# Selective scan in four layers: state tiles of four quarters of n by 32 channels instead of two halves by 64

## The chip, the cores and the metric

The kernel runs on one core of a Trainium2 chip. The metric is the device time of one launch, in microseconds (us); lower is better. The engines are named as in the profile: PE (TensorE matmul), PEld (TensorE weight load), DVE (VectorE), ACT (ScalarE), POOL (GpSimd), SP (SyncE, which here issues every DMA).

## The reference

An image of 8 x 64 x 64 x 96 passes through four layers, each `x = x + f(groupnorm(x))`. Each `f` projects 96 channels to 2 x 192, runs a depthwise convolution with SiLU over the first 192, then a selective scan over the L = 4096 positions with n = 16 states per channel, and after a layer norm (not in the last layer) and a gate `silu(z)` projects 192 channels back to 96. In the first three layers the scan runs in four directions (rows, columns, and each backwards; in the second layer rows and columns are walked in serpentine order) and the results are added. In the fourth it runs once. Cut to what matters here:

```python
dts, Bs, Cs = split(x_proj @ xs)               # rank, 16, 16 rows for each position
delta = softplus(dt_proj @ dts + dt_bias)      # 192 channels
def step(h, (u_t, d_t, b_t, c_t)):             # h is 192 channels x 16 states
    h = exp(d_t[..., None] * A) * h + (d_t * u_t)[..., None] * b_t[None, :]
    y = einsum('dn,n->d', h, c_t)
    return h, y
y = scan(step) + D * xs
```

## The kernel before, in words

The outermost loop runs over the 8 images of the batch, and inside it the four layers are written out. A layer has three stages: the convolution stage (`layer`, up to `by_columns`), the scan stage (`scans`), and the norm stage (`z`, `center`, `spread_`, `norm_`, `out`, `residual`). Everything is fp32, and PE runs each such product as two matmul records.

The scan stage walks chunks of 512 positions: 32 chunks in the first three layers (four directions of eight) and 8 in the last, so 104 for each image and 832 in all. A chunk holds 192 x 16 = 3072 scans of 512 positions, that is 24 scan instructions of 128 rows ("units"). In the kernel before, a unit's 128 rows are two halves of n by 64 channels: rows 0 to 63 hold one state for 64 channels, rows 64 to 127 the state eight further on for the same channels. Four units make a state tile `h` of 128 x 4 x 512; a chunk has `RS` = 6 such tiles, walked as two groups g of four states by three channel tiles t.

For each chunk the work is:

- `project`, `keep_x_dbl`: x_proj on PE gives rank, B and C rows. C and, for the backward directions, all rows go to memory. `load_x_dbl` reads them back there.
- `turn_v`, `softplus`, `delta_of`, `turn_u`, `du_of`: delta and delta*u with positions on the rows (`delta_t`, `du_t`), on PE, ACT, POOL and DVE.
- `spread_b`, `diagonals`: B goes through memory into a 128 x 64 x 64 tile `diag` whose blocks are diagonal matrices of B.
- `turn_back`, `keep_delta`: delta back with channels on the rows. Each of three 64-channel parts is copied from PSUM to one half of a 128 x 512 tile by ACT, and a DMA copies that half to the other half of the rows.
- `enter(q)`: the products `(delta*u)^T diag`, which give delta*u*B for two units at once in a two-bank PSUM tile `dbu`: 16 products with 64 x 64 weights and 128 moving columns each. Two such PSUM tiles exist.
- `decay(m)`: ACT forms exp(delta * A) for unit m, into one of six `d_a` buffers.
- `scan(m)`: DVE runs the recurrence of unit m over 512 positions (`tensor_tensor_scan`).
- `keep(s)`, `read_out(s)`: ACT keeps the last column of a finished state tile, and POOL multiplies the 128 x 2048 tile by C in place. C stands in `cs[i, g]`, two tiles of 1 MB for a chunk, filled by eight DMAs of `spread_c` that repeat each C row over 64 partitions. For the very last tile of a layer DVE does the product in four pieces.
- `add_up(i, e)`: PE sums over n with a 0/1 matrix `sel` of 128 x 64, each time 512 columns, into two PSUM banks `y_ps`; 24 products for a chunk.
- `close_sums(i, o)`: DVE adds `y_ps` to the layer's result, in the order of the direction.

The order on every engine is written out by hand. The loop over m (one m for each unit) emits, in this order: `keep` and `read_out` at every fourth m, `enter(m//2+1)` at every even m, `scan(m)`, `decay(m+4)`, `add_up` at every fourth m, and then what the table `plan` has for the slot `m % 24`. The table places the preparation of the next chunk and the closing of the last; slots are named below as in it. `SL` = 24 slots make a chunk:

```python
        if slot % 4 == 3:
            of, e = divmod(m - 15, SL)
            if 0 <= of < len(walk):
                add_up(of, e // 2)
                add_up(of, e // 2 + 1)
        for do, ahead, *rest in plan.get(slot, ()):
```

All DMAs stand in SP's one queue in program order. The start of a layer's scans (`first_project` to `first_load`) is interleaved with the convolution stage, where `by_two` builds three convolution chunks by pairs of an ACT product (tile `more`, taken by `piece` from the pool `delta` of six buffers) and a POOL addition.

Of the kernel before, what the change touches and what calls it, by code (L numbers as in the profile page):

```python
# [32 lines left out]
NT = 3  # L33
NJ = 8
# [11 lines left out]
NEGMEAN, CEN_B, ONE, EPS, N_CONST = 352, 416, 480, 481, 482  # L46
# [73 lines left out]
def kernel(ctx: ExitStack, tc: tile.TileContext, x_in, const_in, *rest):  # L120
# [3 lines left out]
    def pool(name, bufs, space=None):  # L124
# [9 lines left out]
        cpool=pool("c", 3),  # L134
        upool=pool("u", 4),
        deltas=pool("delta", 6),
# [40 lines left out]
def layer(tc, env, x, stats, x_of, x_to, n, ly):  # L177
# [23 lines left out]
    def piece(name):  # L201
        return env.deltas.tile([128, CH], F32, tag="delta", name=name)
# [329 lines left out]
    with set_of("natural_log_exp_and_others"):  # L532
# [15 lines left out]
        env.cpool.tile([128, 4, CH], F32, tag="c", name="gates"),  # L548
# [147 lines left out]
def scans(tc, env, n, ly, w, u_mem, u_first, d, neg_a, make_ys, two_banks, wide):  # L696
# [9 lines left out]
    sel = const[:, SEL : SEL + 64]  # L706
# [3 lines left out]
    RS, SL = 6, 24  # L710
    halves = [slice(0, 64), slice(64, 128)]
# [14 lines left out]

    def place(s):

        i, r = divmod(s, RS)
        return i, r // NT, r % NT  # L730

# [6 lines left out]
    def u_of(i, half):  # L738
        return u_first(half, 0) if i == 0 else us[i][0 : (128, 64)[half], half, :]

    def load_u(i, part):
        if i >= len(walk):
            return
        k, c = walk[i]
        if part == 0:
            us[i] = env.upool.tile([128, 2, CH], F32, tag="u", name="u")
        s = slice(c * CH, (c + 1) * CH)
        if part == 0:
            nc.sync.dma_start(us[i][:, 0, :], u_mem[k % 2][0:128, s])
        else:  # L750
            nc.sync.dma_start(us[i][halves[part - 1], 1, :], u_mem[k % 2][128:DI, s])

    def project(i, half):
# [8 lines left out]
        for e in range(2):  # L762
            rows = slice(0, 128) if half == 0 else halves[e if i > 1 else 0]
            u = u_first(half, walk[i][1]) if i < 2 else us[i][rows, half, :]
            nc.tensor.matmul(  # L765
                dbls[i][:, e],
                w[rows, at : at + ly.x_rows],
                u[:, e * CH // 2 : (e + 1) * CH // 2],
                start=half == 0,
                stop=half == 1,  # L770
            )

    def keep_x_dbl(i):
# [14 lines left out]
        if i > 1:  # L788
            there = env.deltas.tile([128, CH], F32, tag="delta", name="x_hi")[64 : 64 + XP]
# [17 lines left out]
    def spread_c(i, g, part):  # L807
        k, c = walk[i]
        if part == 0:
            cs[i, g] = env.cpool.tile([128, NH, CH], F32, tag="c", name="c")  # L810
        half, pair = divmod(part, 2)
        rows, js = slice(64 * half, 64 * half + 64), slice(2 * pair, 2 * pair + 2)
        n0 = half * NJ + g * NH + 2 * pair
        of = c_mem[k][n0 : n0 + 2, c * CH : (c + 1) * CH]
        nc.sync.dma_start(cs[i, g][rows, js], of.partition_broadcast(64))
# [5 lines left out]
    def turn_v(i, b):  # L821


        if b == 0:
            for name in ("delta_t", "du_t"):
                turned[i, name] = env.turned.tile([128, NB4, DI], F32, tag=name, name=name)
# [13 lines left out]
    def turn_u(i, b, half):  # L840
# [5 lines left out]
        for b_ in (b, 2 + b):  # L846
# [3 lines left out]
            else:  # L850
                at = halves[b_ // 2 if i > 0 else 0]
                u = us[i][at, 1, :] if i > 0 else u_of(i, 1)
                nc.tensor.transpose(to[:, 128:DI], block(b_, u), ident[at, at])  # L853

    def softplus(i, part):

        v = turned[i, "v"][:, :, 0:DI]
        if part == 0:
            rests[i] = env.turned.tile([128, NB4, DI], F32, tag="rest", name="rest", bufs=1)
# [38 lines left out]
    def turn_back(i, o, part):  # L898
# [3 lines left out]
        for b in (2 * part, 2 * part + 1):  # L902
            of = turned[i, "delta_t"][:, b]
            for half in range(o + 1 if i == 0 else 1):
                to = deltas[i, "ps"][64 * half : 64 * half + 128 // (o + 1), o]
                of_ = of[:, 0:128] if o == 0 else of[:, 128:DI]
                if half == 0:
                    nc.tensor.transpose(block(b, to), of_, ident)  # L908
                else:
                    nc.tensor.matmul(block(b, to), of_, ident, start=True, stop=True)  # L910

    def keep_delta(i, t):

        delta = env.deltas.tile([128, CH], F32, tag="delta", name="delta")
        if i > 0:
            here = halves[t % 2]
            nc.scalar.copy(delta[here], deltas[i, "ps"][here, t // 2])  # L917
            nc.sync.dma_start(delta[halves[1 - t % 2]], delta[here])
        elif t == 2:
            nc.scalar.copy(delta, deltas[i, "ps"][:, 1])  # L920
        else:
            for half in range(2):
                of = deltas[i, "ps"][64 * t : 64 * t + 64, 0]
                nc.scalar.copy(delta[64 * half : 64 * half + 64], of)
        deltas[i, t] = delta


    def enter(q):
# [4 lines left out]
        i, g, t = place(s)  # L933
# [3 lines left out]
        for b in range(NB4):  # L937
            for e in range(2):
                rows = slice(64 * e, 64 * e + 64)
                for half in range(2):  # L940
                    at = b * NS + g * NJ + half * NH + 2 * pair
                    nc.tensor.matmul(  # L942
                        to[64 * half : 64 * half + 64, e, b],
                        du[rows, b, 64 * t : 64 * t + 64],
# [6 lines left out]
    def decay(m):  # L951
# [4 lines left out]
        i, g, t = place(s)  # L956
        d_a = env.decays.tile([128, CH], F32, tag="d_a", name="d_a")
        at = (walk[i][0] * NT + t) * NJ + g * NH + m4
        nc.scalar.activation(d_a, deltas[i, t], AF.Exp, scale=neg_a[:, at : at + 1])  # L959
        decays[m] = d_a  # L960

    def scan(m):
        s, m4 = divmod(m, NH)
        i, g, t = place(s)
# [6 lines left out]
        j = t * NJ + g * NH + m4  # L971
# [10 lines left out]
    def keep(s):  # L982

        i, g, t = place(s)
        at = t * NJ + g * NH
        last = 0 if walk[i][0] >= 2 else CH - 1
        nc.scalar.copy(states[i // NCH][:, at : at + NH], hs[s][:, :, last])  # L987

    def read_out(s):
        i, g, t = place(s)  # L990
        if s < n_s - 1:
            nc.gpsimd.tensor_tensor(hs[s], hs[s], cs[i, g], ALU.mult)  # L992
            return
        for m4 in range(NH):
            of = hs[s][:, m4]
            nc.vector.tensor_tensor(of, of, cs[i, g][:, m4], ALU.mult)

    def add_up(i, e):


        g, e = divmod(e, 6)
        if g == 0 and e == 0:
            sums[i] = [env.ps_y.tile([128, CH], F32, tag=f"y{o}", name=f"y{o}_ps") for o in range(2)]
        s = i * RS + g * NT
        if e < 4:
            work = [(0, 0, s, e), (0, 1, s + 1, e)]
        else:
            work = [(1, 0, s + 2, e - 4), (1, 1, s + 2, e - 2)]
        for o, half, of, state in work:
            nc.tensor.matmul(  # L1010
                sums[i][o][64 * half : 64 * half + 64],
                sel,
                hs[of][:, state, :],
                start=g == 0 and e in (0, 4),
                stop=g == 1 and e in (3, 5),
# [3 lines left out]
    def close_sums(i, o):  # L1019
# [3 lines left out]
        u_ = us[i][:, o, :].rearrange("p (o i) -> p o i", i=W)  # L1023
# [23 lines left out]
        5: [(turn_u, 1, 1, 0), (turn_u, 1, 1, 1)],  # L1047
# [4 lines left out]
        11: [(keep_delta, 1, 2), (close_sums, -1, 0)],  # L1052
        14: [(close_sums, -1, 1)],
# [6 lines left out]
    for at, (do, *what) in (  # L1060
        *((5 + 3 * part, (spread_c, 0, part)) for part in range(4)),
        *((18 + 3 * part, (spread_c, 1, part)) for part in range(4)),
        *((a + 6 + a // 2, (diagonals, a, 1)) for a in range(8)),
    ):
        plan.setdefault(at % SL, []).append((do, 1 - at // SL, *what))
    for part, at in enumerate((1, 2, 4)):
# [15 lines left out]
    def first_softplus(between=lambda: None):  # L1082
# [3 lines left out]
        for part in range(4):  # L1086
            spread_c(0, 0, part)
# [11 lines left out]
    def first_delta():  # L1099
        for t in range(NT):  # L1100
            keep_delta(0, t)

    def first_load():
# [3 lines left out]
        for part in range(4):  # L1107
            spread_c(0, 1, part)
# [10 lines left out]
    for m in range(-8, (len(walk) + 1) * SL):  # L1119
# [10 lines left out]
        if slot % 4 == 3:  # L1130
            of, e = divmod(m - 15, SL)
            if 0 <= of < len(walk):
                add_up(of, e // 2)
                add_up(of, e // 2 + 1)
# [7 lines left out]
def constants():  # L1142
    a = np.zeros((128, N_CONST), np.float32)
    for p in range(128):
        a[p, SEL + p % 64] = 1
        a[p, IDENT + p] = 1
# [11 lines left out]
def pack(ly, conv_w, win, conv_b, x_proj, dt_w, dt_b, a_log, d, w_out, gamma=None, beta=None):  # L1158
# [6 lines left out]
    for k in range(K):  # L1165
# [14 lines left out]
        for half in range(2):  # L1180
            for j in range(NJ):
                a[NS + half * NJ + j, at + DI + j // NH * NJ + half * NH + j % NH] = 1
        a[64 : 64 + XP, at : at + DI + NS] = a[0:XP, at : at + DI + NS]
    a_log = a_log.reshape(K * NT, 64, 2, NJ).transpose(2, 1, 0, 3).reshape(128, -1)
# [55 lines left out]
```

## Time and profile before

| | us |
|---|---|
| median of 3 runs | 29361.2 (29357.19 to 29361.32) |
| the profiled execution, its own time | 29331.35 |
| its span, first to last instruction | 29329.6 |
| mean granted PE clock | 0.98 |

| engine | busy us | share of the span | instructions |
|---|---|---|---|
| PE | 27127.0 | 92% | 391056 |
| DVE | 27395.8 | 93% | 26841 |
| POOL | 25414.1 | 87% | 7101 |
| ACT | 19839.6 | 68% | 35728 |

The shares are averages over three kinds of stage. From the first scan of a layer to the last, the trace has 25195 us in the sum over 32 layers (8 images by 4); the remaining 4135 us lie in the convolution and norm stages. Busy time is the union of an engine's instruction spans; matmul records overlap each other, so a busy PE isn't PE at its peak. The 16 DMA engines are 49% busy in the mean, nearly all of it on SP's queue.

### The profile page before, as it was taken

How to read it: one execution, taken by the hardware profiler on the slowest of the kernel's cores; microseconds unless marked ns; L12 is line 12 of the kernel's file. 1: busy time of each engine (PE TensorE's matmuls, PEld its weight loads, DVE VectorE, ACT ScalarE, POOL GpSimd, SP SyncE). 2: the span in 40 equal slices, each digit the busy share in tenths (PEclk: the TensorE clock that was granted, in tenths of full speed). 3: DMA queues.
4: the chain of work that ended last, by engine and by line, in shares of the span. 5: the costliest groups of instructions: out<-in, count | busy, mean ns of one | idle time of the engine just before them, and what ended most of it. 6: DMA issues, size and time to landing. Idle time of an engine off the chain costs nothing. (4 is left out here: it accounts for less than half of the span.)

```text
span 29329.6 us, 919486 instructions
## 1 busy us (share of the span) xinstructions
PE 27127.0 (92%) x391056; PEld 15249.2 (52%) x391056; DVE 27395.8 (93%) x26841; ACT 19839.6 (68%) x35728; POOL 25414.1 (87%) x7101
## 2 busy tenths in 40 slices
PE   9999999999999999999999999999999999999999
PEld 5555455554555545555455554555545555455554
DVE  9999899998999989999899998999989999899998
ACT  6667666676666766667666676666766667666676
POOL 8898788987889878898788987889878898788987
PEclk9999999999999999999999999999999999999999
DMA  5444454454544545445454454544545455454454
GB/s 132 117 117 125 106 131 117 117 125 106 131 116 118 125 107 130 118 118 125 106 132 117 116 126 107 131 117 116 125 106 131 116 117 125 106 132 117 116 126 106
DMA packets 1947780, 3498.19 MB, mean 119 GB/s; under 512 B 448400, under 2 KB 469264, under 8 KB 1920624
## 3 DMA queue, kind: packets, MB, share of 16 engines
q1 hardware_dynamic: 1943664, 3438.91, 47.7%
q8 instruction: 3120, 51.12, 0.8%
q14 instruction: 996, 8.16, 0.1%
HBM read 2787.17 MB, written 302.84 MB: 105 GB/s over the span
## 5 line engine op out<-in xcount | busy, mean ns | idle before, releaser
L992 POOL TENSOR_TENSOR h<-h,c 128x2048 f32<-128x2048 f32 x4960 | 22450.1, 4567 | 44.5 <-ACT state L987 37.6
L973 DVE TENSOR_TENSOR_SCAN h<-d_a,state,dbu 128x512 f32<-128x512 f32 x17472 | 20778.0, 1274 | 13.0 <-PE dbu L942 6.0
L959 ACT ACTIVATE d_a<-delta,neg_a 128x512 f32<-128x512 f32 x19968 | 13372.2, 719 | 428.1 <-DVE h L973 390.9
L942 PE MATMUL dbu<-diag,du_t 64*64 64x128 f32 x319488 | 11236.9, 275 | 1631.8 <-DVE h L973 1606.6
L942 PEld LDWEIGHTS dbu<-diag,du_t 64*64 64x64 f32 x319488 | 8881.1, 131 | 6556.5 <-issue 5591.6
L1010 PE MATMUL y_ps<-h,const 128*64 128x512 f32 x39936 | 9697.2, 605 | 13.3 <-POOL h L992 13.3
L1010 PEld LDWEIGHTS y_ps<-h,const 128*64 128x64 f32 x39936 | 2441.1, 136 | 3802.9 <-issue 3757.3
L987 ACT COPY state<-h 128x4 f32<-128x4 f32 x4992 | 974.6, 195 | 3692.8 <-DVE h L973 3687.3
L973 DVE TENSOR_TENSOR_SCAN h<-d_a,dbu 128x512 f32<-128x512 f32 x2496 | 2838.3, 1201 | 348.9 <-PE dbu L942 227.6
L877 POOL TENSOR_TENSOR delta_t<-delta_t,rest 128x768 f32<-128x768 f32 x832 | 1525.5, 1834 | 1835.3 <-ACT state L987 1508.3
L917 ACT COPY delta<-delta_ps 64x512 f32<-64x512 f32 x2400 | 1392.3, 580 | 1716.2 <-PE delta_ps L908 1677.1
L832 PE MATMUL v<-w,x_dbl 39*128 39x208 f32 (+1 forms) x5120 | 1388.4, 475 | 33.3 <-ACT x_dbl L781 33.3
L480 POOL TENSOR_TENSOR acc<-acc,more 128x512 f32<-128x512 f32 x576 | 757.4, 1317 | 758.0 <-ACT more L479 724.4
L343 PE MATMUL one_bank<-xn,taps 96*128 96x512 f32 (+1 forms) x2496 | 1220.2, 675 | 22.0 <-DVE taps L219 22.0
L832 PEld LDWEIGHTS v<-w,x_dbl 39*128 39x128 f32 (+1 forms) x5120 | 964.1, 317 | 348.4 <-issue 228.9
L880 DVE TENSOR_TENSOR du_t<-delta_t,u_t 128x768 f32<-128x768 f32 x832 | 782.9, 941 | 162.2 <-POOL delta_t L877 162.2
L871 ACT COPY bt<-v 128x64 f32<-128x64 f32 x832 | 176.5, 212 | 1109.7 <-PE v L832 1108.3
L908 PE MATMUL delta_ps<-const,delta_t 128*128 128x128 f32 (+1 forms) x6656 | 925.6, 280 | 0.0
L1038 DVE TENSOR_TENSOR y<-y,y_ps 128x128 f32<-128x128 f32 (+2 forms) x2048 | 843.9, 457 | 52.0 <-PE y_ps L1010 52.0
L621 POOL TENSOR_TENSOR y<-y,rstd 128x512 f32<-128x512 f32 x192 | 244.3, 1273 | 743.6 <-DVE y L624 531.6
L849 PE MATMUL u_t<-const,u 128*128 128x128 f32 x3328 | 850.3, 338 | 0.0
L343 PEld LDWEIGHTS one_bank<-xn,taps 96*128 96x128 f32 (+1 forms) x2496 | 473.7, 205 | 705.4 <-issue 691.5
(109 smaller groups left out, 15376.3 us busy)
## 6 DMA issues: line engine op xcount, KB each, us to landing
c<-cm SPq DMA_DIRECT2D x3584, 256.0 KB
c<-xm SPq DMA_DIRECT2D x3072, 256.0 KB
diag<-rows SPq DMA_DIRECT2D x6656, 64.0 KB
delta<-delta SPq DMA_DIRECT2D x2400, 128.0 KB
u<-u SPq DMA_DIRECT2D x1088, 256.0 KB
u<-u SPq DMA_DIRECT2D x1920, 128.0 KB
u<-u SPq DMA_DIRECT2D x48, 1024.0 KB
x_dbl<-xm SPq DMA_DIRECT2D x512, 78.0 KB
```

The source lines that it names most:

```text
L343: nc.tensor.matmul(part, taps[:, t, d0 : d0 + nd], rhs, start=t == 0, stop=t == ly.taps - 1)
L832: nc.tensor.matmul(turned[i, "v"][:, 2 * e + b], block(2 * e + b, of), w[o : o + XP, at : at + DI + NS], start=True, stop=True,)
L849: nc.tensor.transpose(to[:, 0:128], block(b_, u_of(i, 0)), ident)
L877: nc.gpsimd.tensor_tensor(delta_t, delta_t, rests.pop(i), ALU.add)
L908: nc.tensor.transpose(block(b, to), of_, ident)
L917: nc.scalar.copy(delta[here], deltas[i, "ps"][here, t // 2])
L942: nc.tensor.matmul(to[64 * half : 64 * half + 64, e, b], du[rows, b, 64 * t : 64 * t + 64], diag[rows, :, at : at + 2], start=True, stop=True,
L959: nc.scalar.activation(d_a, deltas[i, t], AF.Exp, scale=neg_a[:, at : at + 1])
L973: nc.vector.tensor_tensor_scan(hs[s][:, m4, flow], decays.pop(m)[:, flow], p[:, flow], 0.0 if first else states[i // NCH][:, j : j + 1], A ...
L987: nc.scalar.copy(states[i // NCH][:, at : at + NH], hs[s][:, :, last])
L992: nc.gpsimd.tensor_tensor(hs[s], hs[s], cs[i, g], ALU.mult)
L1010: nc.tensor.matmul(sums[i][o][64 * half : 64 * half + 64], sel, hs[of][:, state, :], start=g == 0 and e in (0, 4), stop=g == 1 and e in (3 ...
```

## The change

A unit's 128 rows become four quarters of n (`NQ` = 4, `NJ` = 4 states each) by 32 channels (`DQ` = 32; six channel tiles, `NT` = 6). A state tile still has four units, now two channel tiles by two states, in the order `groups`. What follows from it:

- `enter`: 32 products with 64 x 32 weights for two units, instead of 16 with 64 x 64; the moving columns stay 128.
- `add_up`: `sel` is 128 x 32, and four products at a time go to the four quarters of a PSUM bank. There are still 24 for a chunk, four at every fourth m as before.
- `spread_c`: one tile of 128 x 4 x 512 for the chunk, 1 MB, filled by four DMAs. `read_out` reads it with a repeated dimension, once for each of the two channel tiles.
- `keep_delta`, `spread_delta`: ACT copies the whole of delta in two copies (128 and 64 rows), two DMAs write it to memory (384 KB), and eight DMAs of 192 KB read it back, repeated over the four quarters. `turn_back` of the first chunk no longer makes a second copy of its 64-row part.
- Buffers: `c` 3 to 2, `u` 4 to 3 and 4 for its two halves (now separate tiles), `delta` 6 of 128 x 512 to 4 of 128 x 3 x 512 (also those of `piece`), `delta_t` 2 to 1; `rest`, the stored delta and `x_hi` share one buffer `passing`. The third `gates` tile of the norm stage comes from the pool `h` instead of `c`.
- The plan: `close_sums` moves from slots 11 and 14 to 5 and 13, `load_u` from 1, 2, 4 to 6, 1, 2; the spreads of delta stand in slots 12 to 15 and 17 to 20, those of C in 8, 13, 18, 23.

The diff, cut to its core:

```diff
+NQ = 4
+DQ = 32
+NT = DI // DQ
+NJ = NS // NQ
...
-        cpool=pool("c", 3),
-        upool=pool("u", 4),
-        deltas=pool("delta", 6),
+        cpool=pool("c", 2),
+        upool=pool("u", 3),
+        deltas=pool("delta", 4),
...
     def piece(name):
-        return env.deltas.tile([128, CH], F32, tag="delta", name=name)
+        return env.deltas.tile([128, 3, CH], F32, tag="delta", name=name)[:, 0]
...
+    groups = [(0, 0), (1, 0), (0, 1), (1, 1), (2, 0), (2, 1)]
...
+    def spread_c(i, q):
         k, c = walk[i]
+        if q == 0:
+            cs[i] = env.cpool.tile([128, NJ, CH], F32, tag="c", name="c")
+        of = c_mem[k][q * NJ : q * NJ + NJ, c * CH : (c + 1) * CH]
+        nc.sync.dma_start(cs[i][DQ * q : DQ * q + DQ], of.partition_broadcast(DQ))
...
+    def keep_delta(i, o):
+        if o == 0:
+            deltas[i, "sb"] = passing("delta_sb").rearrange("p (o l) -> p o l", o=2)
+            deltas[i, "mem"] = env.dram.tile([DI, CH], F32, tag="delta", name=f"delta{i}_{n}", bufs=2)
+        rows = slice(0, 128 // (o + 1))
+        nc.scalar.copy(deltas[i, "sb"][rows, o], deltas[i, "ps"][rows, o])
+        at = slice(0, 128) if o == 0 else slice(128, DI)
+        nc.sync.dma_start(deltas[i, "mem"][at], deltas[i, "sb"][rows, o])
+
+    def spread_delta(i, part, q):
+        if q == 0:
+            deltas[i, part] = env.deltas.tile([128, 3, CH], F32, tag="delta", name="delta")
+        of = deltas[i, "mem"].rearrange("(t r) l -> r t l", r=DQ)[:, 3 * part : 3 * part + 3]
+        nc.sync.dma_start(deltas[i, part][DQ * q : DQ * q + DQ], of)
...
-                for half in range(2):
-                    at = b * NS + g * NJ + half * NH + 2 * pair
+                for q_ in range(NQ):
+                    at = b * NS + q_ * NJ + 2 * pair_j
                     nc.tensor.matmul(
-                        to[64 * half : 64 * half + 64, e, b],
-                        du[rows, b, 64 * t : 64 * t + 64],
+                        to[DQ * q_ : DQ * q_ + DQ, e, b],
+                        du[rows, b, at_d : at_d + DQ],
                         diag[rows, :, at : at + 2],
...
+        c = cs[i][:, 2 * pair_j : 2 * pair_j + 2]
         if s < n_s - 1:
-            nc.gpsimd.tensor_tensor(hs[s], hs[s], cs[i, g], ALU.mult)
+            h = hs[s].rearrange("p (t j) l -> p t (j l)", j=2)
+            c = c.rearrange("p j l -> p (j l)").unsqueeze(1).to_broadcast([128, 2, 2 * CH])
+            nc.gpsimd.tensor_tensor(h, h, c, ALU.mult)
...
         if e < 4:
-            work = [(0, 0, s, e), (0, 1, s + 1, e)]
+            work = [(0, s + e // 2 * 2 + t // 2, t % 2 * 2 + e % 2) for t in range(4)]
         else:
-            work = [(1, 0, s + 2, e - 4), (1, 1, s + 2, e - 2)]
-        for o, half, of, state in work:
+            work = [(1, s + e, t * 2 + j) for j in range(2) for t in range(2)]
+        for at, (o, of, unit) in enumerate(work):
             nc.tensor.matmul(
-                sums[i][o][64 * half : 64 * half + 64],
+                sums[i][o][DQ * at : DQ * at + DQ],
                 sel,
...
-                add_up(of, e // 2)
-                add_up(of, e // 2 + 1)
+                add_up(of, e // 4)
```

## The prediction

> **What bounds the kernel now.** I read the page first, part 5: who is busy, and whether anything waits for it. Columns: line, engine, operation, operands and count, then busy us and mean ns of one, then the engine's idle time just before and what ended most of it.
>
> ```profile
> PE 27127.0 (92%) x391056; PEld 15249.2 (52%) x391056; DVE 27395.8 (93%) x26841; ACT 19839.6 (68%) x35728; POOL 25414.1 (87%) x7101
> ...
> L992 POOL TENSOR_TENSOR h<-h,c 128x2048 f32<-128x2048 f32 x4960 | 22450.1, 4567 | 44.5 <-ACT state L987 37.6
> L973 DVE TENSOR_TENSOR_SCAN h<-d_a,state,dbu 128x512 f32<-128x512 f32 x17472 | 20778.0, 1274 | 13.0 <-PE dbu L942 6.0
> ...
> L942 PE MATMUL dbu<-diag,du_t 64*64 64x128 f32 x319488 | 11236.9, 275 | 1631.8 <-DVE h L973 1606.6
> ...
> L1010 PE MATMUL y_ps<-h,const 128*64 128x512 f32 x39936 | 9697.2, 605 | 13.3 <-POOL h L992 13.3
> ```
>
> Three engines look alike, but 17472 scans waited 13 us in all, while PE waited 1606.6 us for the scans. Next I took busy time by stretch, for one steady chunk (slot 0 to the next slot 0; columns: length, then busy us of PE, PEld, DVE, ACT, POOL with counts, PE clock, DMA share, GB/s):
>
> ```profile
> 2078.40:2108.99 30.59, 28.04 (x458) 16.57 (x456) 30.59 (x34) 20.82 (x38) 28.73 (x8) 1.00 0.49 116
> ```
>
> DVE is busy 30.59 of 30.59 us. Its scans start every 1.171 us in the trace (the 1274 ns overlap the next): 24 make 28.1, `du_of` and the two closings the rest. POOL has 6 x 4.567 + 1.834 = 29.2, PE 28.0. So a scan stage ends when DVE ends, and nothing taken from PE, POOL or the DMAs there shortens it. All DVE waits inside the 32 scan stages come to 120 us in the trace, 54 of them in the first chunks. A gain must come from there, or from the 4135 us outside, where PE leads in stretches. So I looked at PE's timeline where a layer's scans end (start, length, what; idle before):
>
> ```profile
> 2166.44 2.79 PE L1010 MATMUL y_ps<-h,const 128*64 128x512 f32 x10
> 2169.65 5.36 PE L1010 MATMUL y_ps<-h,const 128*64 128x512 f32 x22 [0.42 <-POOL h L992]
> 2174.94 1.98 PE L567 MATMUL z_a<-xc,w 96*128 96x512 f32 x4
> ```
>
> The last products of `add_up` run without a gap into the norm stage, and PE stays busy to about 2195: that end is PE's.
>
> **The change, part by part.** Sums are made against the profiled execution (29331.35, its span 29329.6), which is 0.1% below the median of 29361.2; I subtract from the median.
>
> *Sums by four strips.* Now 8 records for four products take 1.87 us from start to start, with two 64-column strips at work together. Bounds: 1.87 if four strips don't overlap better than two, 0.93 if they do. I take 0.93, as the two strips now do overlap: two records start within 7 ns of each other and the next two 429 ns later. In the scans PE goes from 28.0 to 28.0 - 6 x 0.93 = 22.4 us a chunk, worth nothing under DVE. At a layer's end: POOL has tile s+4 at 2169.6, DVE's last piece is ready at 2172.1, so the last four products end near 2172.9 instead of 2175.0 and `z` starts about 2.0 us earlier (`xc` needs x, which landed at 2172.1 and comes about 0.9 earlier, as its buffers are freed by a shorter `add_up`). 32 x 2.0 = **-64 us** (bounds 0 and -90).
>
> *Products of 64 x 32.* A group for two units takes 1.05 us now: 32 records, eight rounds. In the trace of the group at 2013.16 four matmuls start at .327, .332, .340 and .349, the next four at .439 to .459: a round of four takes 110 ns, and its starts only 22. So columns set the pace, not the issue, and eight in a round would start within 50 to 60 ns. Bounds: 1.05 us (eight side by side in the same 110 ns) and 2.1 (a record costs 33 ns whatever its width). I take 1.05, by the row of starts. The chunk's sum stays at 22.4; each group has two scans (2.34 us) in which to be made, so nothing is exposed.
>
> [...]
>
> *C in 1 MB, POOL.* Four DMAs less and 1 MB less a chunk. POOL's product has as many elements, so I take 4.567 us; a repeated operand isn't in the trace. Bounds: 0 and, by L480's 1317 ns for 512 elements (2.57 ns each against 2.23), +15%. POOL has 1.1 to 1.4 us of 30.6 free, so up to +4% costs nothing.
>
> *Delta through memory.* Three SP issues with 64-row copies become two writes and eight reads, against four C issues less: 28 a chunk instead of 25, at 0.34 to 0.6 us each, 16 of 30.6 us. ACT saves one 580 ns copy, free time anyway. The new wait is on SP: the first `spread_delta` stands until the second write has landed, and behind it wait four of the eight `diagonals` of the next chunk, one C, two `x_dbl`. SP now:
>
> ```profile
> 2093.50 0.50 SPq L918 DMA_DIRECT2D delta<-delta  x1
> ...
> 2100.02 0.81 SPq L896 DMA_DIRECT2D diag<-rows  x2
> ```
>
> The write that takes that 2093.50 place lands 2.2 to 3.9 us later (the three of this chunk did), say at 2096.5. Then eleven issues of 0.55 us put the last diagonal at 2102.6, and it lands by 2105 to 2107 (these landings took 2.1 to 4.9 us). PE needs it at 2106.9 for the group before the next chunk's first scan at 2109.0, at the latest at 2107.9. Delta itself is due by 2108.3 and lands near 2104. So it fits with 1 to 3 us to spare: 0.
>
> *Layer starts.* PE drops four L910 copies, at a step of 0.37 us, from an unbroken run of PE up to 2298.5 that the first scan waits for: -1.5. Four `more` buffers instead of six: in `by_two(1)`, POOL adds one each 1.33 us, ACT writes one each 0.63, so ACT's eighth product waits for the fourth addition (2269.7 instead of 2268.5), which is before `keep_x_dbl` and PE's `turn_v`: +1.1 in the 24 image layers. Eight reads before the big u stores: +0.5 (0 to 3). Together 32 x (-1.5 + 0.5) + 24 x 1.1 = **-6 us** (-48 to +75).
>
> *Stalls inside the scans.* Some of the 120 us are PE arriving late behind `add_up` (1.5 us at 2327, in a first chunk). I take a good third, **-50 us** (0 to -120).
>
> Sum: -64 - 6 - 50 = -120, so 29361 - 120 = **29240 us**; this case's own range is 29120 to 29330.
>
> **The rivals.** 0.2% (59 us) is about what a measurement of this kernel can tell from no change.
>
> *Issue sets the pace after all (slower).* Place: `enter`. If a record costs what it does now in busy time, 11236.9 / 319488 = 35 ns, a group grows by 32 x 35 = 1.1 us, and PE needs 22.4 + 12 x 1.1 = 36 us a chunk against 30.6: 832 x 5.2 = +4300 us, 33,700. It decides from the point where a group takes 0.68 us more than now (8.2 us a chunk over 12 groups), that is 1.73 us; at 1.85 it is +1.4 us a chunk, 30,500. For: no 64 x 32 product is in the trace, and no long run at under 27 ns a record. Against: the rounds above. 0.13.
>
> *The diagonals come late (slower).* If the last diagonal lands at 2108.9 instead of 2107.9, DVE waits 1 us in every chunk: 832 us, 30,150. For: the third delta issue already stood 1.66 us on SP in this chunk, because a DMA waits for the one eight issues before it. Against: the spare time worked out above. With smaller lateness this case reaches down to 29,500. 0.13.
>
> *PE's clock.* The trace grants half the clock for 3.4 us after a stretch with little matmul work. In a first chunk (columns as above):
>
> ```profile
> 2318.50:2321.90 3.40, 1.52 (x47) 1.34 (x51) 3.40 (x4) 3.25 (x7) 3.40 (x2) 1.00 0.87 204
> 2321.90:2325.30 3.40, 3.40 (x34) 1.61 (x27) 3.40 (x4) 1.90 (x5) 3.40 (x2) 0.50 0.60 157
> ```
>
> 1.52 busy us were too few. Behind the closing in slot 13 such a stretch will now arise in scan stages, since `add_up` is halved. At half clock two groups and a sum need 6.1 us for four scans of 4.7, which the gaps before and after take up once; if it came in every other stretch, DVE would lose about 1.5 us a chunk, 30,600. 0.05.
>
> *POOL slower by over 4%*: at +6%, 0.6 us a chunk, 29,860. 0.04.
>
> *No difference*: ends and starts cancel, within 29,300 to 29,420. 0.15.
>
> The forecast has 0.50. Cases of both signs hold most of the chance, so the range takes in small and middling lateness: 29,120 to 30,200; outside lie the greater part of the issue case, the clock case and some of the diagonals, about 0.17.
>
> Chances: faster 0.50, same 0.15, slower 0.13 + 0.13 + 0.05 + 0.04 = 0.35.
>
> **What would show it.** Right: chunks of 30.6 us with DVE at 100%; L942's group still 1.05 us from start to start with 64 records, `y_ps` 0.93; PE near 22 us a chunk; `z` about 2 us sooner after the last scan; the DVE idle before scans below the present 13 and 349 us. Wrong: DVE waiting for PE dbu in every chunk (issue, if the group is long; diagonals, if PE waits for a DMA; clock, if the granted clock falls), or L992 above 4.75 us.

## The result: slower, and the profile after

| | us |
|---|---|
| before, median of 4 runs beside it | 29361.3 (29357.2 to 29365.4) |
| after, median of 4 runs | 31920.6 (31878.9 to 31991.3) |
| ratio after to before, 95% interval | 1.0874 (1.0854 to 1.0894) |
| the profiled execution after, its own time and span | 31911.08, 31909.3 |

The forecast was 29,240 in a range of 29,120 to 30,200. The change costs 2560 us. From the page of the changed kernel (columns as for the page before):

```profile
PE 25670.4 (80%) x710288; PEld 14684.6 (46%) x710288; DVE 27581.0 (86%) x26841; ACT 19462.5 (61%) x34832; POOL 25550.1 (80%) x7101
...
L1005 POOL TENSOR_TENSOR h<-h,c 128x2048 f32<-128x2048 f32 x4960 | 22565.7, 4581 | 903.1 <-ACT state L997 377.5
L982 DVE TENSOR_TENSOR_SCAN h<-d_a,state,dbu 128x512 f32<-128x512 f32 x17472 | 20884.3, 1259 | 2081.5 <-PE dbu L948 1551.6
L948 PE MATMUL dbu<-diag,du_t 64*32 64x128 f32 x638976 | 13156.8, 284 | 5267.7 <-DVE h L982 2680.9
```

No engine is full any more. POOL's product is as long as before (4581 ns against 4567), and PE has less to do (80% against 92%), yet the scans wait 2081.5 us where they waited 13, mostly for PE. The windows show the same by chunk (slot 0 to slot 0):

```profile
2091.25:2123.18 31.93, 26.45 (x848) 16.14 (x840) 30.72 (x33) 20.03 (x36) 28.73 (x7) 0.95 0.53 137
2155.20:2189.22 34.02, 24.94 (x844) 15.13 (x840) 30.89 (x33) 20.14 (x37) 30.65 (x8) 1.00 0.53 129
```

DVE still has its 30.8 us of work, but the chunk takes 32 to 34 us, differing from one to the next, and it does so with the clock at 1.00 as well. By the starts and ends of the scans in the two traces, the 32 scan stages grew from 25194.8 to 27775.6 us: 2581 us, the whole of the difference. DVE's waits inside them grew from 120 to 2528 us.

PE's timeline in the first of those chunks tells where PE is late:

```profile
2105.97 1.07 PE L1022 MATMUL y_ps<-h,const 128*32 128x512 f32 x8
2107.22 0.86 PE L948 MATMUL dbu<-diag,du_t 64*32 64x128 f32 x40 [0.19 <-DVE h L982]
2109.01 1.71 PE L948 MATMUL dbu<-diag,du_t 64*32 64x128 f32 x88 [0.93 <-issue]
2110.65 1.07 PE L1022 MATMUL y_ps<-h,const 128*32 128x512 f32 x8
2112.73 0.67 PE L948 MATMUL dbu<-diag,du_t 64*32 64x128 f32 x31 [1.01 <-DVE h L982]
2114.97 2.44 PE L948 MATMUL dbu<-diag,du_t 64*32 64x128 f32 x85 [1.58 <-issue]
```

A group has 64 records. The one that starts at 2107.22 stops after 40 of them, the one at 2112.73 after 31, and then PE stands 0.93 and 1.58 us for "issue", that is for nothing that the profile shows: these products have no semaphore to wait for. The scans that need the second group start at 2116.13, 1.20 us late. In the list of PE's waits this is now the second largest item, where before it was 0.2 us:

```profile
PE dbu L948 <- DVE h L982: 2680.9, 3575, 3.0
PE dbu L948 <- issue: 2478.5, 2076, 5.0
```

What PE stands for shows in part 3 of the page: the queue that brings PE its instructions. Before and after (packets, MB, share of 16 engines):

```profile
q8 instruction: 3120, 51.12, 0.8%
```

```profile
q8 instruction: 5608, 91.88, 1.3%
```

A packet has 16 KB (91.88 MB in 5608). PE's 710288 matmul and 710288 weight-load records and 14,186 others, divided by 5608 packets, are 256 instructions to a packet. In the changed kernel's trace the packets near the two stops landed at 2107.63 and 2113.31; PE went on 1.38 and 1.66 us later. Over all stops of more than 0.3 us inside groups (2260, together 3273 us) the time from the packet's landing to the next instruction is 1.25 to 1.67 us (5% to 95%, median 1.44), and from its start 2.64 us. Numbering PE's instructions in the order of the trace settles it: the 219 stops of over 0.7 us in the first image's groups all fall on the same place modulo 256, within one instruction (those of each other image, 190 and more in every one, likewise on a place of their own). PE stops where a block of 256 instructions ends and the next has not come. At the ends of 2609 of 5599 blocks there is a gap of over 0.3 us, in front of whatever instruction. In the kernel before there was one such gap in the groups.

A product in fp32 leaves two weight loads and two matmuls on the queue at either width: of each kind the trace has 319488 records for the 832 x 12 x 16 products of 64 x 64, and 638976 for twice as many of 64 x 32. A group of 16 products is 64 instructions, one of 32 is 128. So PE uses up a block in 3.1 to 5.9 us in the changed kernel (5% to 95%, median 4.4, the gap at its end left out), and in 7.3 to 9.8 us (median 8.3) in the first image of the kernel before. The packet of the next block starts 1.7 us (median; 0.7 to 4.1) after PE enters a block, and 2.64 us later PE can go on: 4.3 us together. The block between the two stops above was used up in 4.11 us; the packet for the next one started 3.41 us after PE had entered it. Of the 254 blocks used up in under 3 us 233 ended in a gap, of the 1283 that took 5 us or more 271. In the first image, when a packet starts, the first instruction that needs it is 216 ahead in the kernel before (median; 279 at the 99th percentile) and 137 in the changed one; when it lands, 185 and 74.

Late packets go with busy DMA engines. Where these were under 10% busy in the first microsecond after PE entered a block, the next packet started 1.17 us after that (median), and 377 of 1416 blocks ended in a gap; where they were 90% busy or more, it was 2.66 us, and 816 of 1060. That is read from the changed kernel's trace; no run tests it.

Of DVE's 2528 us of waits inside the scan stages of the changed kernel, 2339 follow within 5 us of such a gap.

### The profile page after: what moved, and what is told of

It is laid out like the page before. It is cut to its first block, busy times and chain, and to the rows that moved or that the text cites. A ratio compares the mean times of both kernels' runs of the same rounds, so it can differ in the third digit from the quotient of the medians.

```text
span 31909.3 us, 1561566 instructions
## 1 busy us (share of the span) xinstructions
PE 25670.4 (80%) x710288; PEld 14684.6 (46%) x710288; DVE 27581.0 (86%) x26841; ACT 19462.5 (61%) x34832; POOL 25550.1 (80%) x7101
## 3 DMA queue, kind: packets, MB, share of 16 engines
q8 instruction: 5608, 91.88, 1.3%
## 4 chain that ended last, share of the span: by engine, by line
## 5 line engine op out<-in xcount | busy, mean ns | idle before, releaser
L1005 POOL TENSOR_TENSOR h<-h,c 128x2048 f32<-128x2048 f32 x4960 | 22565.7, 4581 | 903.1 <-ACT state L997 377.5
L982 DVE TENSOR_TENSOR_SCAN h<-d_a,state,dbu 128x512 f32<-128x512 f32 x17472 | 20884.3, 1259 | 2081.5 <-PE dbu L948 1551.6
L948 PE MATMUL dbu<-diag,du_t 64*32 64x128 f32 x638976 | 13156.8, 284 | 5267.7 <-DVE h L982 2680.9
L948 PEld LDWEIGHTS dbu<-diag,du_t 64*32 64x32 f32 x638976 | 9849.4, 108 | 11604.1 <-issue 7395.7
L1022 PE MATMUL y_ps<-h,const 128*32 128x512 f32 x39936 | 5909.4, 650 | 200.1 <-issue 143.7
L921 ACT COPY delta_sb<-delta_ps 128x512 f32<-128x512 f32 (+1 forms) x1664 | 959.2, 578 | 1213.2 <-PE delta_ps L913 1188.4
L840 PE MATMUL v<-w,x_dbl 39*128 39x208 f32 (+1 forms) x5120 | 1456.6, 496 | 132.0 <-issue 74.7
L1022 PEld LDWEIGHTS y_ps<-h,const 128*32 128x32 f32 x39936 | 843.7, 111 | 1470.1 <-issue 1291.1
L774 PE MATMUL x_dbl<-u,w 64*103 64x256 f32 (+3 forms) x3584 | 837.9, 422 | 79.2 <-issue 29.8
```

What stands on the lines that cost most here:

```text
L840: nc.tensor.matmul(turned[i, "v"][:, 2 * e + b], block(2 * e + b, of), w[o : o + XP, at : at + DI + NS], start=True, stop=True,)
L921: nc.scalar.copy(deltas[i, "sb"][rows, o], deltas[i, "ps"][rows, o])
L948: nc.tensor.matmul(to[DQ * q_ : DQ * q_ + DQ, e, b], du[rows, b, at_d : at_d + DQ], diag[rows, :, at : at + 2], start=True, stop=True,)
L982: nc.vector.tensor_tensor_scan(hs[s][:, m4, flow], decays.pop(m)[:, flow], p[:, flow], 0.0 if first else states[i // NCH][:, j : j + 1], A ...
L1005: nc.gpsimd.tensor_tensor(h, h, c, ALU.mult)
L1022: nc.tensor.matmul(sums[i][o][DQ * at : DQ * at + DQ], sel, hs[of][:, unit, :], start=e in (0, 4), stop=e in (3, 5), skip_group_check=True,)
```

## Experiments

T1: PE's instruction stream, doubled, comes too slowly. T2: less array work lets PE's clock fall, and the groups come late. T3: delta through memory or late diagonals. T4: a product of 64 x 32 is slower in the array. Medians; ratios are to the runs of the kernel before beside them (29364 to 29372).

**1. The kernel before with its products split, nothing else.**

```diff
-                for half in range(2):
+                parts = 2 if True else 1
+                wd = 64 // parts
+                for o in range(2 * parts):
+                    half = o // parts
...
+                    ch = 64 * t + o % parts * wd
...
-                        to[64 * half : 64 * half + 64, e, b],
-                        du[rows, b, 64 * t : 64 * t + 64],
+                        to[wd * o : wd * o + wd, e, b],
+                        du[rows, b, ch : ch + wd],
```

> The kernel before, with each 64x64 product with B issued as two 64x32 products (32 products a group for 16); tiles, sums, C, delta and all DMAs stay. Instruction stream theory (T1: TensorE's doubled instruction stream is fetched too slowly): about 5616 instruction packets of 16 KB instead of 3120, stops of 1 us and more in the middle of product groups, DVE waiting for dbu, at least the loss of the changed kernel, 31,700 to 34,000 us, since TensorE has 28.0 busy us of 30.6 here and so less room to catch up. Clock theory (T2: less array work halves the clock): the array work of a chunk is as before, so 29,360. Transfer theory (T3: delta through memory, or late diagonals): nothing moved, so 29,360. Product theory (T4: a 64x32 product itself takes longer in the array): as slow as the changed kernel, but by groups that are long from start to end, not by stops.

32776.6 us, ratio 1.116 (1.114 to 1.118). The split alone makes the loss, with delta, C and every DMA as before and the clock at 0.972: against T2 and T3. But it isn't T1 alone. A group took 1075 ns from its first to its last start (median) against 848 before and 904 in the changed kernel; that is 12 x 0.23 = 2.7 us a chunk on a PE that was busy 28.0 of 30.6. Why these groups are longer than those of the changed kernel, with products of the same shape, is open. Of DVE's 3061 us of waits 1624 follow within 5 us of a gap at a block's end, 1437 do not.

**2. The changed kernel with 16 wide products.**

```diff
-                for q_ in range(NQ):
+                for q_ in range(0, NQ, 2):
...
+                    ch = min(at_d, DI - 2 * DQ)
...
-                        to[DQ * q_ : DQ * q_ + DQ, e, b],
-                        du[rows, b, at_d : at_d + DQ],
+                        to[DQ * q_ : DQ * q_ + 2 * DQ, e, b],
+                        du[rows, b, ch : ch + 2 * DQ],
```

> The changed kernel with 16 products of 64x64 a group instead of 32 of 64x32: each covers two quarters of n with the one quarter's columns, so half of the state gets the wrong B and channels (left out: the right values of two quarters); all else as changed. T1: about 3112 instruction packets, no stops inside groups, DVE waits in the scan stages back near 100 us, 29,200 to 29,450. T2: the array work is no larger than in the changed kernel (the sums are halved all the same), the clock falls as often, 31,000 to 31,900. T3: delta, C and the SP order are those of the changed kernel, so 31,900. T4: 29,200 to 29,450, as T1.

29472.7, ratio 1.0032 (1.0019 to 1.0044). All of the change is still there but the number of products, and 2448 of the 2559 us are gone:

```profile
q8 instruction: 3112, 50.99, 0.8%
...
L983 DVE TENSOR_TENSOR_SCAN h<-d_a,state,dbu 128x512 f32<-128x512 f32 x17472 | 20741.3, 1263 | 234.5 <-PE dbu L949 214.6
```

T3 falls for the steady chunks, and T2 for the most part: the array has no more work than in the changed kernel. The 105 us that remain above the kernel before put the run 23 us over T1's range, and T1's "no stops" was a miss: 165 stops of over 0.3 us are left inside groups, 175 us in all, though a block lasts 7.0 us or more here (5th percentile). What remains is mostly elsewhere. Of the 317 us that DVE waits in the scan stages of this trace (120 before), 95 stand ahead of a single scan, the first of a layer's second chunk, some 4 us in each of the 24 image layers; in the kernel before that scan never waits. PE waits there for `x_hi`, a second copy of the third chunk's rank and B rows, which `turn_v` reads; the group that the scan needs stands behind that in PE's order:

```profile
PE v L840 <- DMA x_hi<-x_dbl: 77.6, 28, 5.6
```

The kernel before has no such wait. In its image layers this copy is issued 0.03 us after its source is ready, and PE's product starts 3.5 us later; in run 2 it is 1.1 to 2.1 us and another 4.9 to 5.6 (medians). It now stands among the reads of delta on SP and shares the buffer `passing`; which of the two holds it up, no run separates. Another 70 us of the waits follow within 5 us of a gap at a block's end. For the clock see run 12.

**3. The changed kernel with B, du_t and the diagonals in fp16**, so that a product is one load and one matmul.

```diff
-                    [128, NB4, DI], F32, tag=name, name=name, bufs=bufs
+                    [128, NB4, DI], of, tag=name, name=name, bufs=bufs     # du_t: F16
-        env.wts.tile([128, 64, NB4 * NS], F32, tag=f"diag{o}", name=f"diag{o}") for o in range(2)
+        env.wts.tile([128, 64, NB4 * NS], F16, tag=f"diag{o}", name=f"diag{o}") for o in range(2)
```

> The changed kernel with du_t, B and the diagonals kept in fp16: the 32 products of 64x32 stay in number and shape, but each is one weight load and one matmul instead of two and two (values rounded to fp16). T1: about 3112 instruction packets, no stops, 29,150 to 29,450. T2: each product does half of the array work, so the clock falls more often than in the changed kernel, 31,900 to 33,500. T3: diagonals of half the bytes, delta as changed: 31,000 to 31,900. T4: if the 64x32 shape is what costs, half of the loss at most comes back, 30,600.

29301.2, ratio 0.9978 (0.9968 to 0.9987): 0.2% under the kernel before, with 32 products of 64 x 32 in every group.

```profile
q8 instruction: 3080, 50.46, 0.8%
...
L983 DVE TENSOR_TENSOR_SCAN h<-d_a,state,dbu 128x512 f32<-128x512 f32 x17472 | 20725.6, 1267 | 72.2 <-PE dbu L949 46.0
L949 PE MATMUL dbu<-diag,du_t 64*32 64x128 f16 x319488 | 6585.3, 288 | 6629.8 <-DVE h L983 6605.0
```

The mean clock is 0.769, far below the 0.931 of the changed kernel, and the run is 0.2% under the kernel before all the same. T4 falls as far as the shape goes: the same 32 products, with half the instructions, are in time.

**4. The changed kernel with a filler for the clock**: ahead of each group

```diff
+        nc.tensor.matmul(p[:, 0:256], ident, const[:, 0:256], start=True, stop=True)
```

> The changed kernel with one 128x128 product of 256 columns ahead of each group, written into the group's own tile and overwritten by the group: array work that keeps the clock up, for 4 more instructions in 128. T2: the clock stays near 1.00 in the scans and the time comes back to 29,300 to 29,900 (TensorE 27.5 busy us of 30.6). T1: no gain; TensorE has 0.4 us less for each group, 31,900 to 33,500, with the stops inside groups as many as in the changed kernel even where the clock is whole. T3: 31,900.

32742.9, ratio 1.1148. The clock rose from 0.931 to 0.962. The stops inside groups fell by half (1059, 1594 us, against 2260 and 3273), where T1 had as many as before, and the time rose by 822 us; but run 12 shows that the filler itself costs some 800 us, so this one says little alone.

**5. Run 3 with two idle weight loads ahead of each product.**

```diff
+                    for _ in range(2):
+                        nc.tensor.ldweights(du[rows, b, at_d : at_d + DQ], tile_position=(64 * e, DQ * q_))
```

> The changed kernel in fp16 of the third run, with two idle weight loads (the product's own weights, 64x32) ahead of each product: three loads and one matmul, 128 instructions a group as in the changed kernel, while array work, tiles, DMAs and results stay as in the third run. T1: about 5580 instruction packets, stops inside groups, 31,000 to 32,800 us. If what cost the time was the matmuls themselves, or the clock: 29,300 to 29,500, since no matmul is added.

39499.5: not what any theory said. The loads were meant to be only instructions, but each takes its turn: a group lasts 1759 ns from first to last start against 365 in run 3, (1759 - 365) / 64 = 22 ns a load. PE is busy 97% of the span. As a test of T1 it failed, with one lesson: 5576 packets came, nearly as many as in the changed kernel, 6.5 us apart, and there were some 50 stops of over 0.3 us in the groups, against 2260. It isn't the number of packets alone that costs.

**6. Half of the blocks split in the kernel before.** Against run 1:

```diff
-                parts = 2 if True else 1
+                parts = 2 if b % 2 == 0 else 1
```

> The kernel before, with the products of two of the four blocks b split in two as in the first run: 24 products and 96 instructions a group instead of 64. T1: about 4368 instruction packets, one for each 6 to 7 us; between 29,360 and the 32,780 of the whole split. If the loss goes with the number of packets, half of it: 31,070. If it has a threshold (a fetch takes 2.6 us from its start until TensorE goes on), less than a third: 29,400 to 30,500, with the stops in the busiest slots only.

33973.2, slower than the whole split, which no expectation had. The groups took 1444 ns, and 30,021 times a load came more than 0.3 us after the one before it (median 364 ns), three to a group and not at block ends: there, products of 64 x 64 and 64 x 32 follow each other. PE pays for each change of shape: by the groups, 1444 against 962, the middle of 848 and 1075, is 482 ns for three changes, 0.16 us each. The gap between the loads at a change is 0.36 us, more than twice what the group grows by at each.

**11. Every second group split, all of its blocks**, to take that out.

```diff
-                parts = 2 if b % 2 == 0 else 1
+                parts = 2 if pair == 0 else 1
```

> The kernel before with the products split in two in every second group (all of its blocks), so that the shape of tile doesn't change inside a group: the same 4368 packets as the half split of the sixth run, whose groups took 1444 ns from first to last start against 848 before and 1075 in the whole split, by some 360 ns at each change between 64x64 and 64x32. If the change of shape made that run slower than the whole split: 29,700 to 31,100 here. If it was the fetch: 33,970 again.

30478.2, ratio 1.0375 (1.0358 to 1.0393). Run 6's 3500 us more, with the same 4368 packets, were the changes of shape. With groups of one shape, half of the split costs 1114 of the whole split's 3409 us, a third: it rises faster than in proportion. In PE's timeline the two kinds of group stand side by side, 1.11 and 1.38 us long:

```profile
2060.84 1.11 PE L946 MATMUL dbu<-diag,du_t 64*64 64x128 f32 x32
2063.14 1.38 PE L946 MATMUL dbu<-diag,du_t 64*32 64x128 f32 x64 [1.18 <-DVE h L977]
```

**9 and 10. Run 3 with two, then one, no-operation behind each product.**

```diff
+                    for _ in range(2):          # run 10: range(1)
+                        nc.tensor.nop("pad", nofuse=True)
```

> The third run's kernel (fp16, 64 instructions a group) with two no-operation instructions on TensorE's queue behind each product: 128 instructions a group as in the changed kernel, with no weight load and no matmul added. T1: about 5580 instruction packets; stops inside groups, at one place in every 256 instructions; 30,800 to 32,800 us. If the loss came from the products themselves: 29,300.

> As the run before it, with one no-operation behind each product: 96 instructions a group, about 4330 instruction packets. T1 with a threshold (a packet is needed each 7 us, and one takes 2.6 us): 29,350 to 30,200, few stops. T1 in proportion: half of the loss of 128 instructions, 30,000 to 31,100. Products: 29,300.

60063.5 and 39055.8. A no-operation is anything but free: groups last 3528 and 1774 ns, (3528 - 365) / 64 = 49 and (1774 - 365) / 32 = 44 ns each, and PE is the bound at 98 to 99%. Neither tests T1. There are no long stops at block ends; at this pace a block lasts 10.3 and 8.2 us.

**7. The kernel before in fp16**, as run 3 (the diagonals, their rows in memory and `bt` likewise).

```diff
-            for name in ("delta_t", "du_t"):
-                turned[i, name] = env.turned.tile([128, NB4, DI], F32, tag=name, name=name)
+            for name, of in (("delta_t", F32), ("du_t", F16)):
+                turned[i, name] = env.turned.tile([128, NB4, DI], of, tag=name, name=name)
```

> The kernel before with du_t, B and the diagonals in fp16, nothing else: what fp16 is worth without the new tiles. TensorE has fewer instructions and less work, but VectorE bounds the scan stages: 29,250 to 29,370. If the third run's gain of 0.22% came from fp16 alone, this is as fast as the third run or faster (29,300 or below); if it came from the four-strip sums at the layers' ends (24 starts and 32 ends, about 57 us), this stays at 29,360.

29309.3, ratio 0.9980 (0.9971 to 0.9989). fp16 alone brings what run 3 brought. With the instruction stream out of the way the new tiles are worth 29301 - 29309 = -8 us, within the runs' spread: nothing that these runs can tell from zero.

**8. Run 3 with the loads of u behind the first delta.**

```diff
-            early.load()
             early.turn_back()
...
             early.keep_delta()
+            early.load()
```

> The third run's kernel with the first two chunks' loads of u issued behind, not ahead of, the first chunk's delta writes and reads in the 24 image layers. In the changed kernel's trace these loads keep SyncE from 5280.85 to 5285.8 us while delta_sb is ready at 5280.5, and ACT waits 2.38 us for delta ahead of the first scan. Expected: delta lands some 4 us earlier, the first scan 0.5 to 1.5 us earlier until TensorE's own run sets it: 24 x 1 = 25 us less, 29,275 (29,240 to 29,310). If delta was not what the first scan waits for: 29,301.

29311.5, the same as run 3. In the trace the step itself came out: from the last scan of a layer to the first of the next image layer it takes 1.3, 1.5 and 1.1 us less than in run 3, some 30 us in 23 starts. But the waits up to the first scan of the second chunk rose from 100 to 137 us, and the start of the fourth layer, which the edit doesn't touch, took 1.8 us longer. It was given back; why there, I did not follow.

**12. Run 2 with run 4's filler**, to see whether the clock is what was left there.

```diff
+        nc.tensor.matmul(p[:, 0:256], ident, const[:, 0:256], start=True, stop=True)
```

> The second run's kernel (16 products of 64x64 a group, two quarters of n with the wrong B and channels) with one 128x128 product of 256 columns ahead of each group, overwritten by it. The second run stayed 0.3% above the kernel before, and in its trace 255 of the 339 us that VectorE waits in the scan stages come after stretches at half the clock with no stop of TensorE's stream before them. If the clock is what was left: the clock near 1.00 in the scan stages, those waits gone, 29,230 to 29,370. If it was delta through memory, or SyncE's order: 29,470. If the 0.4 us more of TensorE's work for each group matter: above 29,500.

30274.1, ratio 1.0307. The waits within 5 us of half clock fell from 249 to 111 us, but PE's busy time rose by 5051 us, 0.51 for each group, to 95% of the span, and the waits with neither half clock nor a stop near rose from 38 to 639 us. So the run doesn't settle by its time how much of run 2's 105 us is the clock. Its trace says something: the wait ahead of the second chunk's first scan is still 86 us. In run 2 half clock came within 5 us of that wait's end, but not ahead of its start: there PE's idling comes first. Behind half clock with neither that wait nor a stop near stand 116 us of run 2's waits (32 in the kernel before); that is read, not shown by an experiment.

## Why the prediction was wrong, point by point

**Wrong: the products of 64 x 32.** The step that failed is "each group has two scans (2.34 us) in which to be made, so nothing is exposed". The price was right: groups that don't stop take 904 ns from first to last start against 848, 1.10 to 1.16 us in step with 64 records, inside the bounds and next to the 1.05 taken. So the rival "issue sets the pace", whose range the time fell into, is not what happened: the number fits it by luck. What was left out is that 64 more instructions a group must first reach PE. I costed the 64 records in the array and at the issue, and not at their source, though the queue stood in part 3 of the page with 3120 packets, one each 9.4 us of the span. Doubling the products was to add 832 x 12 x 64 / 256 = 2496 packets; 2488 came. The term is +2448 us by run 2, where the sum had 0; in run 3, the same tiles in fp16, it is gone too.

How late the packets come could have been counted in the trace of before: in its first image 99 of 100 start at most 279 instructions ahead of need, little more than a block. There the crossing of a block was hidden, with one gap inside the groups; in the changed kernel it was not, with gaps at the ends of 2609 of 5599 blocks.

The upper bound of 2.1 us took a record to cost 33 ns whatever its width. 64 records in 1.10 us are 17 ns each, so that didn't come, as argued from the row of starts. But issue was not the only thing upstream of the array.

**Right: sums by four strips.** Eight `y_ps` records take 1.00 us from start to the next start against 1.87; 0.93 was taken. PE's sum for a chunk was still too low: 26.3 us busy in the chunks at full clock (median) for 22.4, which is under DVE's 30.6 all the same. At the layers' ends `z` starts 3.79 us after the last scan instead of 5.57, 32 x 1.78 = -57 us for -64 forecast. Where the second layer ends:

```profile
2385.75 3.56 PE L1022 MATMUL y_ps<-h,const 128*32 128x512 f32 x16 [1.84 <-POOL h L1005]
2389.24 1.98 PE L569 MATMUL z_a<-xc,w 96*128 96x512 f32 x4
```

PE now waits 1.84 us for POOL's last tile there, and still hands over to `z` at 3.79 us after the scans.

**Mis-sized: layer starts**, -6 us with bounds of -48 and +75. From `z` to the next first scan it takes 4.1, 0.9, -0.6 and 2.8 us more after the four layers, some +55 us over the 31 starts, which eats the gain at the ends. Ahead of the second layer's first scan, ACT's and SP's timelines show one reason:

```profile
5280.85 0.33 SPq L758 DMA_DIRECT2D u<-u  x1
5282.03 1.27 SPq L760 DMA_DIRECT2D u<-u  x2
5283.35 0.58 SPq L758 DMA_DIRECT2D u<-u  x1
5284.68 1.08 SPq L760 DMA_DIRECT2D u<-u  x2
5285.87 1.04 SPq L923 DMA_DIRECT2D delta<-delta_sb  x2
5288.87 3.63 SPq L930 DMA_DIRECT2D delta<-delta  x8
```

```profile
5294.23 3.17 ACT L966 ACTIVATE d_a<-delta,neg_a 128x512 f32<-128x512 f32 x5 [2.38 <-DMA delta<-delta]
```

`delta_sb` was ready at 5280.5, but its write stands on SP behind six loads of u; I had priced the eight reads, and not what the writes queue behind. Another is PE's clock: in the same stage 12 records of the convolution take 8.17 us at a granted clock of 0.65, where they took 5.42 at 1.00.

**Not seen: stalls inside the scans**, -50 forecast. In run 3, where the stream isn't in the way, DVE waits 151 us against 120: 46 more up to the first scan of the second chunk, 16 less elsewhere. That scan alone waits 63 us, where it waited nothing: the late `x_hi` of run 2.

**Right: C and POOL, delta in time.** L1005 has 4581 ns. Delta through memory doesn't bound a steady chunk: runs 2 and 3 have it and lose 0.3% and nothing. It was worked out for a steady chunk alone; in a layer's first chunk the copy of `x_hi` among its reads is late (run 2). One reason given for the rival of late diagonals doesn't hold. In the trace of before 20,715 of SP's 21,843 issues do wait for the semaphore of the DMA eight issues before them; but the third delta issue stood 1.66 us from 2094.86, and the DMA eight issues before it had landed at 2089.04. What held it the trace doesn't show.

**The clock rival** came in small. In the changed kernel 157 us of waits come behind half-clock stretches with no stop near, and another 1447 behind both a stop and half clock. For half of these (724 us) there was no half clock in the 5 us before the wait began, so it may lengthen what the stops begin; how much of the 1447 us is the clock's, no run separates. Run 3, at a clock of 0.769 and 0.2% under the kernel before, shows that a low clock alone cost nothing where PE had the room.

The chances were off for the reason that misled the sum: 0.35 for slower, none of it for the instruction queue.

## What to carry to other kernels

Splitting a matmul into narrower ones costs instructions even where the array runs them side by side at little cost (904 ns for a group here against 848). Count the bytes of an engine's instruction stream as any other transfer: here 256 instructions a packet, a median of 1.7 us from PE's entering a block to the start of the next packet, more where the DMA engines are busy (2.66 us at 90% and more, 1.17 under 10%), and 2.64 us from there until PE goes on. Blocks used up in 7.3 to 9.8 us left one gap in the groups of the kernel before; blocks used up in 3.1 to 5.9 us cost 2448 us in the changed one. The mark in a profile is an engine that stops for "issue" in the middle of instructions that have nothing to wait for, with the instruction queue's packets up.

## What the runs showed of the hardware that was not expected

- In the changed kernel PE stopped at the end of 2609 of 5599 blocks of 256 instructions, within an image at the same place modulo 256, and went on 1.44 us after the next packet landed (1.25 to 1.67). The packet started late where the DMA engines were busy: 2.66 us after PE enters a block at 90% and more, 1.17 us under 10%.
- A change between 64 x 64 and 64 x 32 products left 0.36 us between weight loads and lengthened a group by 0.16 us (run 6); keeping a group to one shape took 3495 us off the run (run 11).
- An idle 64 x 32 weight load cost 22 ns (run 5), and a no-operation on PE's queue 44 to 49 ns (runs 10 and 9), more than a 64 x 32 product's share of a group in fp16 (365 / 32 = 11 ns).
- With a mean clock of 0.769 run 3 took 0.2% less than the kernel before at 0.98: where DVE was the bound, PE's granted clock said little.
